# Banded product on four 64x64 tiles of TensorE, with half of the channels kept with swapped row halves, and a new order within a step

## The chip, the cores and the metric

The kernel runs on one core of one Trainium2 chip. The metric is the device time in microseconds; times of a kernel agree within a few tenths of a per cent. Matrix products run on TensorE (PE), which also loads weights (PEld in the profile); VectorE (DVE), ScalarE (ACT) and GpSimd (POOL) do the elementwise work, and SyncE (SP) starts the DMA transfers. All data is 32-bit floating point, and each matrix product of this type appears in the profile as a pair of records for the loads and a pair for the products (a transpose as one).

## The reference, cut to what matters

Two layers of the same form run one after the other on an image x of 512 x 512 positions with 64 channels:

```
xn    = layer_norm(group_norm(x))                       # 64 channels
left  = (xn @ Wl + bl) * mask * sigmoid(xn @ Wlg + blg)  # 128 channels
right = (xn @ Wr + br) * mask * sigmoid(xn @ Wrg + brg)
gate  = sigmoid(xn @ Wog + bog)
out[i, j, h] = sum over r with |r - i| <= 4 of left[r, i, h] * right[r, j, h]
x     = x + (layer_norm(out) * gate) @ Wo + bo
```

The sum over r is a matrix product for each of the 128 channels h: a band matrix (rows i, columns r, nine diagonals) times the columns j of `right`. `left` is needed only near the diagonal of the image.

## The kernel before, in words

**Tiling.** The 512 rows are cut into 9 blocks of 64 rows that overlap by 8. A block's 512 columns are taken as two halves of 256, which lie one above the other on the 128 partitions: partitions 0 to 63 hold the block's rows for columns of the left half, partitions 64 to 127 the same rows for the right half. A chunk is 128 columns of each half, so a layer has 18 chunks. A chunk is worked on in 16 steps, and each step takes one unit of 8 columns per half.

**What a unit goes through.** SP loads it (`load`, L390). Group norm is applied as a multiplication and an addition (`affine`, L426, on POOL, two instructions). DVE takes its statistics (`inner_stats`, L431). Every fourth step a `solve` (L577) turns the statistics of some units and outputs into reciprocal standard deviations: five small DVE instructions, then a chain of twelve on POOL. POOL subtracts and multiplies (`inner_norm`, L435). PE transposes the unit (`transposed`, L441), ACT copies the transposed unit to `zT` and adds 1, the row that carries the biases being folded in this way (`kept`, L460), and SP also writes it to DRAM (`later`). A step later, `right` (L487) multiplies `zT` with the weights of right and its gate in two calls of four columns: PE writes two banks of PSUM, ACT takes the sigmoid of one half of the channels into `sg`, and DVE multiplies it with the other half into `RO`, the array of 128 channels x 240 columns that holds the right side, and then, in place, the output of the band product.

**The left side.** At the head of a layer, the 36 near-diagonal columns go through the same way in five units (`left`, L497, at steps 3, 5, 7, 9, 11). ACT, POOL and DVE build the values in `sg`, and SP writes them from there into the DRAM array `left_of` in slabs of 16 channels, 108 transfers per layer. `left_of` has been filled with zeros, so reading it with another stride (`take_left`, L527) gives full 64 x 64 band matrices: tile `A`, 16 channels at a time, by two transfers of 256 KB.

**The band product.** `mix` (L539) takes 8 channels: for each of them, and each of the two halves, a product of a 64x64 matrix with 64x128 of `RO`. The lower half's products use rows and columns 0 to 63 of the array, the upper half's 64 to 127:

```
hh = (turn ^ e) * (HB // 2) + h
en.tensor.matmul(
    ph[part, hh, :], lhsT=A[part, :, h0 % HA + hh],
    rhs=R[part, (h0 + hh) // 2, :, hh % 2],
```

The result fills two banks; ACT copies the first half back into `RO`, DVE the second. A chunk has 16 such products, spread over its first ten steps as 2, 1, 2, 2, 1, 2, 1, 2, 2, 1; the other six steps have none.

**The output.** Some 14 steps after its band product starts, a unit of output has had its statistics taken (`out_stats`, L571, four DVE instructions) and solved; ACT normalises it in eight instructions into `on` (`norm`, L610; one buffer), PE turns it (`turned`, L641), PE and ACT make the output gate from the transposed input read back from DRAM (`gates`, L622; `recall`, L618), DVE adds the bias and multiplies by the gate into `ZH`, PE multiplies with Wo (`end`, L673), and DVE adds that to the residual `XR`, to which POOL has added the output bias (`biased`, L667). SP writes it. In layer 1, PE also sums the result for the next group norm (`sums`, L692, into its own bank `acc`).

**What sets the order.** Every instruction of a step is issued through the class `InOrder` (L365), which keeps program order on each engine; this is why nearly all profile rows carry L373, and why groups are told apart by their tiles. The order of a step in `layer` (L704) is: three output statistics, affines, first `right`, more statistics, `gates`, second `right`, `left`, `inner_norm`, `turned` with its multiplication, `transposed` and `kept`, `biased`, the rest of the statistics, `end`, `sums`, the solve, `norm` of the next output, and last the band products with their copies. Each engine takes its own part of this list, strictly in turn; SP does so too, with about nine transfers a step. PSUM has eight banks: two buffers of two banks (`two_banks`: both `right` calls, `transposed`, `mix`), and single banks (`one_bank`: `gates`, `turned`, `end`), three in layer 1 and four in layer 2.

Of the kernel before, what the change touches and what calls it, by code (L numbers as in the profile page):

```python
# [16 lines left out]
P = 128  # L17
WIN = 4
# [61 lines left out]
def tile_two_banded_layers(  # L80
# [28 lines left out]
    slab = S * (S + 2 * WIN) * HA  # L109
    size = H // HA * slab  # L110
# [271 lines left out]
    class Unit:  # L382
# [4 lines left out]
        def __init__(self, at: int, blk: Block = None, j: int = 0, near: int = None):  # L387
            self.at, self.blk, self.j, self.near = at, blk, j, near

# [70 lines left out]
    def kept(u: Unit):  # L460
        u.t = ztp.tile([P, JU // 2, P], F32, tag="zT", name="zT")
        to = u.t.rearrange("c k (n p) -> c n k p", n=2)
# [5 lines left out]
        if u.near is None:  # L468
            en.sync.dma_start(later[u.at], u.t)
# [5 lines left out]
    def projected(u: Unit, q: int, w: bass.AP):  # L475

        pr = two_banks().rearrange("p (e k h) -> p e k h", e=2, k=JQ // 2)
        for k in range(JQ // 2):
            for e in range(2):
                part = slice(e * D, (e + 1) * D)  # L480
                en.tensor.matmul(
                    pr[:, e, k, :], lhsT=u.t[part, q // 2 + k, :], rhs=w[part],
                    start=True, stop=True,
                )
        return pr

    def right(u: Unit, q: int, w: dict):  # L487
        pr = projected(u, q, w["right"]).rearrange("p e k h -> p (e k) h")
        sg = wk.tile([P, JQ, H], F32, tag="sg", name="sg", bufs=2)
        en.scalar.activation(sg, pr[:, :, H:], AF.Sigmoid)  # L490
        en.vector.tensor_tensor(
            RO[:, :, u.c + q : u.c + q + JQ, :],
            pr[:, :, :H].rearrange("p j (h t) -> p h j t", t=2),
            sg.rearrange("p j (h t) -> p h j t", t=2), ALU.mult,
        )

    def left(u: Unit, q: int, w: dict):  # L497
# [4 lines left out]
        sl = sg.rearrange("p j h -> p (j h)").rearrange("p (s j x) -> p s j x", j=JQ, x=HA)  # L502
        sv = sl.rearrange("p s (k e) x -> p e k s x", e=2)
        for e in range(2):
            en.scalar.activation(
                sv[:, e], pr[:, e, :, H:].rearrange("p k (s x) -> p k s x", x=HA), AF.Sigmoid
            )
        near = w["near"][:, n0 : n0 + JQ].unsqueeze(1).unsqueeze(3)
        en.gpsimd.tensor_tensor(sl, sl, near.broadcast_to([P, H // HA, JQ, HA]), ALU.mult)
        for e in range(2):  # L510
            en.vector.tensor_tensor(
                sv[:, e], pr[:, e, :, :H].rearrange("p k (s x) -> p k s x", x=HA), sv[:, e],
                ALU.mult,
            )
        for o, r, k, m in runs(n0, n0 + JQ):
            for n, b in enumerate(blocks):
                q0 = b.s // JQ
                at = n * size + (r * (S + 2 * WIN + 1) + k) * HA
                en.sync.dma_start(
                    strided(  # L520
                        left_of, at, (JQ * (S + 2 * WIN + 1) * HA, S // JQ), (slab, H // HA),
                        (1, m * HA),
                    ),
                    sl[q0 : q0 + S // JQ, :, o : o + m, :].rearrange("q s j x -> q s (j x)"),
                )

    def take_left(n: int, h: int) -> bass.AP:  # L527


        A = lp.tile([P, S, HA], F32, tag="A", name="A")  # L530
        at = n * size + h * slab + WIN * HA
        for e in range(2):
            en.sync.dma_start(
                A[e * S : (e + 1) * S].rearrange("p i h -> p (i h)"),
                strided(left_of, at, ((S + 2 * WIN) * HA, S), (1, S * HA)),
            )
        return A

    def mix(c: int, A: bass.AP, h0: int):  # L539


        j0 = c % 2 * (JC - JW)
        R = RO[:, :, j0 : j0 + JC, :]
        pb = two_banks()
        ph = pb.rearrange("i (h j) -> i h j", j=JC)
        for turn in range(2):
            for h in range(HB // 2):
                for e in range(2):
                    part = slice(e * S, (e + 1) * S)
                    hh = (turn ^ e) * (HB // 2) + h  # L550
# [431 lines left out]
```

## Time and profile before

| | |
|---|---|
| runs | 4960.42, 4958.66, 4958.12 us; median 4958.66 |
| span of the profiled execution | 4957.7 us |
| busy, share of the span | PE 84%, PE weight loads 71%, DVE 77%, ACT 74%, POOL 77% |
| DMA queue of SP | 899840 packets, 969.73 MB, 66.9% of 16 engines |
| band product, PE | 18432 records of 64x128, mean 277 ns (overlapping), 1154.3 us busy |
| projections, PE | 9360 records of 64x256, mean 405 ns, 1325.0 us busy |
| copies of the band product | 576 on ACT, 583 ns; 576 on DVE, 691 ns |
| zT copies on ACT | 542 of 128x512, 598 ns; 88 of 128x256, 385 ns |
| POOL, per unit | affine 1283 + 1282 ns, norm 1070 + 1055 ns, residual bias 1190 ns |

The median of the runs is 0.96 us above the span of the profiled execution. The shares are means over the whole span, which begins with some 300 us of group statistics and of zero filling, and has a drain and a refill between the layers, near 2500 to 2800 us; a stretch of the middle of a layer is the better guide. Busy times on PE count overlapping products once, so the pace of PE is read from the starts of its groups. A wait is written as the engine that waited, the releaser, the total in us, how often, and the longest.

### The profile page before, as it was taken

Reading aid. Unit: us, or ns where it says so; the run is one execution under the profiler, and the core shown is the slowest. Engines: PE = TensorE matmul, PEld = TensorE weight load, DVE = VectorE, ACT = ScalarE, POOL = GpSimd, SP = SyncE. Lnnn points to the kernel's source line nnn. Section 1 sums busy time; section 2 is a strip of 40 time slices with the busy share of each in tenths; the row PEclk is TensorE's granted clock in tenths of the full one; section 3 lists DMA queues with packets and bytes.
Section 4 is the critical chain, followed back from the end, with each engine's and each line's share of the span. In section 5 each row is a group of like instructions: output and inputs, shape, how many; then the busy total and the mean of one; then the engine's idle time right before and its main releaser. Section 6 shows DMA issues by size and latency. Waiting matters only on the chain. (4 is left out here: it accounts for less than half of the span.)

```text
span 4957.7 us, 173298 instructions
## 1 busy us (share of the span) xinstructions
PE 4186.4 (84%) x67090; PEld 3543.6 (71%) x67090; DVE 3836.3 (77%) x9635; ACT 3645.2 (74%) x8156; POOL 3826.5 (77%) x4739
## 2 busy tenths in 40 slices
PE   1036899999999999999974689999999999999998
PEld 0025788888888888888763577777777777777775
DVE  6855788888888888888766578888888888888876
ACT  0013788888888888888872378888888888888888
POOL 0037888888888888888534788888888998889853
PEclk6558999999999999999996899999999999999999
DMA  7844677777777777777653467777777777777765
GB/s 305 338 156 130 182 203 207 204 207 204 204 203 204 205 206 206 202 207 210 187 143 88 129 181 205 202 207 205 203 206 202 205 206 205 208 207 209 209 184 152
DMA packets 905343, 982.32 MB, mean 198 GB/s; under 512 B 114210, under 2 KB 641608, under 8 KB 900168
## 3 DMA queue, kind: packets, MB, share of 16 engines
q1 hardware_dynamic: 899840, 969.73, 66.9%
q8 instruction: 531, 8.70, 0.8%
q14 instruction: 292, 2.39, 0.2%
q10 hardware_dynamic: 4680, 1.50, 0.1%
HBM read 658.42 MB, written 312.46 MB: 196 GB/s over the span
## 5 line engine op out<-in xcount | busy, mean ns | idle before, releaser
L373 ACT ACTIVATE on<-RO,nm,rs 128x128 f32<-128x128 f32 x4608 | 1872.5, 496 | 130.1 <-POOL nm L373 110.3
L373 PE MATMUL banks<-pack,zT 64*128 64x256 f32 x9360 | 1325.0, 405 | 148.6 <-DVE RO L373 67.8
L373 PEld LDWEIGHTS banks<-pack,zT 64*128 64x128 f32 x9360 | 886.7, 194 | 517.6 <-DVE RO L373 220.1
L373 PE MATMUL banks<-RO,A 64*64 64x128 f32 x18432 | 1154.3, 277 | 12.7 <-ACT zT L373 12.7
L373 DVE TENSOR_TENSOR RO<-banks,sg 128x512 f32<-128x512 f32 x1152 | 789.9, 686 | 421.1 <-ACT sg L373 402.9
L373 PEld LDWEIGHTS banks<-RO,A 64*64 64x64 f32 x18432 | 1082.3, 183 | 38.6 <-ACT zT L373 15.2
L373 ACT ACTIVATE sg<-banks 128x512 f32<-128x512 f32 (+1 forms) x1188 | 695.0, 587 | 372.5 <-PE banks L373 288.6
L373 DVE BATCH_NORM_STATS2 sto<-RO 128x6 f32<-128x256 f32 x2304 | 842.8, 413 | 1.2
L373 DVE SCALAR_TENSOR_TENSOR ZH<-bank,pack,gate 128x448 f32<-128x448 f32 (+1 forms) x1152 | 738.4, 683 | 71.5 <-ACT gate L373 46.9
L373 DVE COPY RO<-banks 128x512 f32<-128x512 f32 x576 | 396.3, 691 | 487.6 <-ACT RO L373 487.0
L373 POOL TENSOR_TENSOR z<-z,gb 128x512 f32<-128x512 f32 x536 | 687.1, 1282 | 42.0
L373 PE MATMUL bank<-pack,ZH 128*64 128x64 f32 x18432 | 682.8, 229 | 6.1 <-ACT gate L373 5.6
L373 POOL TENSOR_TENSOR z<-z,ga 128x512 f32<-128x512 f32 x536 | 687.8, 1283 | 0.1
L373 POOL TENSOR_TENSOR z<-z,rs 128x512 f32<-128x512 f32 x586 | 618.0, 1055 | 46.0
L373 PEld LDWEIGHTS bank<-pack,ZH 128*64 128x64 f32 x18432 | 602.1, 141 | 48.2 <-ACT gate L373 9.6
L373 POOL TENSOR_TENSOR z<-z,sti 128x512 f32<-128x512 f32 x586 | 627.2, 1070 | 0.0
L373 ACT ACTIVATE gate<-bank 128x448 f32<-128x448 f32 (+1 forms) x1152 | 565.9, 543 | 81.1 <-PE bank L373 66.9
L373 PEld LDWEIGHTS bank<-ident,on 64*128 64x128 f32 x9216 | 409.7, 140 | 260.5 <-ACT gate L373 145.3
L373 PE MATMUL bank<-ident,on 64*128 64x64 f32 x9216 | 450.2, 227 | 137.9 <-ACT gate L373 107.3
L373 PE MATMUL bank<-zg,pack 64*128 64x448 f32 (+1 forms) x2304 | 559.5, 558 | 2.2 <-DMA zg<-later 1.5
L373 POOL TENSOR_TENSOR XR<-XR,pack 120x512 f32<-120x512 f32 (+1 forms) x352 | 418.4, 1190 | 160.6 <-DMA XR<-in_x_dram 58.9
L373 ACT COPY RO<-banks 128x512 f32<-128x512 f32 x576 | 333.5, 583 | 234.1 <-PE banks L373 234.0
(145 smaller groups left out, 3683.3 us busy)
## 6 DMA issues: line engine op xcount, KB each, us to landing
later<-zT SPq DMA_DIRECT2D x576, 256.0 KB
A<-left_of SPq DMA_DIRECT2D x576, 256.0 KB
zg<-later SPq DMA_DIRECT2D x576, 256.0 KB
z<-in_x_dram SPq DMA_DIRECT2D x576, 128.0 KB
z<-mid_x SPq DMA_DIRECT2D x576, 128.0 KB
gn_x<-in_x_dram SPq DMA_DIRECT2D x16, 4096.0 KB
XR<-in_x_dram SPq DMA_DIRECT2D x448, 112.0 KB
mid_x<-XR SPq DMA_DIRECT2D x448, 112.0 KB
```

Source lines behind the costliest of these rows:

```text
L373: return lambda *a, **k: tc.keep_in_program_order(f(*a, **k))
```

## The change

- `mix` takes 4 channels of the lower 64 and 4 of the upper 64 instead of 8 neighbours. The lower ones (s = 0) are multiplied as before; for the upper ones (s = 1) the products go to the other half's output partitions, so that the four 64x64 tiles are addressed in turn. Each s has a single bank of its own (`one_bank`, no longer `two_banks`). `mix` only issues the products; the copies are placed in the step by the caller.
- So that this adds up, the upper 64 channels of `RO` are kept with swapped row halves after one band product, and before it: `crossed` replaces `projected` for the right side and makes 8 products of 128 columns per call in place of 4 of 256. Half of them use weights that begin 64 columns further into `zT`, which therefore gets a third block, a copy of its first, by one more ACT instruction per unit in `kept`. The transfer to `later` takes only the first two blocks.
- The left side is kept as channel pairs: DVE writes it to `L9`, the last 36 columns of `RO`, and each of the four rows of diagonals goes out in 9 transfers when it is complete, with pieces of 18 values. `A` is read back in four transfers of 128 KB with pieces of 128 values.
- `right`, `gates`, `turned`, `norm`, `end` are cut into a PE part and the parts of ACT or DVE, and a step has a new order.

```
 def kept(u: Unit):
-    u.t = ztp.tile([P, JU // 2, P], F32, tag="zT", name="zT")
+    u.t = ztp.tile([P, JU // 2, P + S], F32, tag="zT", name="zT")
...
     if u.near is None:
-        en.sync.dma_start(later[u.at], u.t)
+        en.scalar.activation(
+            to[:, 2], u.pt[0][:, 0].rearrange("c (k p) -> c k p", p=S), AF.Identity, bias=1.0
+        )
+        en.sync.dma_start(later[u.at], u.t[:, :, :P])
...
+def crossed(u: Unit, q: int, w: bass.AP):
+    pr = two_banks().rearrange("p (e k h) -> p e k h", e=2, k=JQ // 2)
+    for k in range(JQ // 2):
+        for s in range(2):
+            for e in range(2):
+                part = slice(e * D, (e + 1) * D)
+                en.tensor.matmul(
+                    pr[:, e, k, :].rearrange("p (g s x) -> p g s x", g=2, s=2)[:, :, s],
+                    lhsT=u.t[part, q // 2 + k, s * S : s * S + P],
+                    rhs=w[part].rearrange("c (g s x) -> c g s x", g=2, s=2)[:, :, s],
+                    start=True, stop=True,
+                )
+    return pr
...
 def take_left(n: int, h: int) -> bass.AP:
+    A = lp.tile([P, HA // 2, S, 2], F32, tag="A", name="A")
+    q = HA // 4
+    for e in range(2):
+        for s in range(2):
             en.sync.dma_start(
+                A[e * S : (e + 1) * S, s * q : (s + 1) * q].rearrange("p h i t -> p h (i t)"),
                 strided(
+                    left_of, n * size + (s * H // 4 + h * q) * span + 2 * WIN,
+                    (H // 2 * span, S), (span, q), (1, 2 * S),
                 ),
             )
...
 def mix(c: int, A: bass.AP, h0: int) -> list:
+    R = RO.rearrange("p (s h) j t -> p s h j t", s=2)[:, :, h0 // 4 : h0 // 4 + q, j0 : j0 + JC]
+    L = A.rearrange("p (s h) i t -> p s h i t", s=2)[:, :, h0 % HA // 4 : h0 % HA // 4 + q]
+    ph = [one_bank().rearrange("i (h t j) -> i h t j", h=q, t=2) for s in range(2)]
+    for h in range(q):
+        for t in range(2):
+            for s in range(2):
+                for e in range(2):
+                    part, to = (slice(n * S, (n + 1) * S) for n in (e, e ^ s))
+                    en.tensor.matmul(
+                        ph[s][to, h, t, :], lhsT=L[part, s, h, :, t], rhs=R[part, s, h, :, t],
+                        start=True, stop=True,
+                    )
+    return [(R[:, s], ph[s].rearrange("i h t j -> i h j t")) for s in range(2)]
```

The new order of a step, with the engine that each entry occupies (transfers and conditions left out):

```
left; out_stats 0:3 (DVE); inner_norm (POOL)
right first half (PE); right_gate (ACT); gates (PE); right second half (PE)
affine (POOL); out_stats 3: (DVE); inner_stats (DVE); solve (DVE, POOL)   # solve every fourth step
gated (ACT); right_end first half (DVE); biased (POOL); turned (PE); right_gate second half (ACT)
transposed (PE); times_gate (DVE); affines of the next step after a solve (POOL); end (PE)
right_end second half (DVE); first mix (PE); norm 0:4 (ACT); kept (ACT); sums (PE)
copy of the first mix, s = 0 (ACT); ended (DVE); norm 4:8 (ACT); second mix (PE)
copy of the first mix, s = 1 (DVE); copies of the second mix (ACT, DVE)
```

## Prediction

> **What bounds the kernel now.** I read the page's first parts, then one 500 us stretch of the middle of layer 1 (busy times, waits), then the timeline of single steps on TensorE, ScalarE and GpSimd. Busy share first:
>
> ```profile
> 1500.00:2000.00 500.00, 481.14 (x8307) 421.74 (x8304) 403.75 (x1019) 418.52 (x934) 445.16 (x539) 0.99 0.72 205
> ```
>
> In steady state PE is busy 96%, POOL 89%, ACT 84%, DVE 81%, the DMA engines 72%, at full clock. Nothing has much room, so what a faster PE is worth depends on the next engine. One step with two band products (`mix`), and the start of the following one, on PE:
>
> ```profile
> 1509.70 1.13 PE L373 MATMUL banks<-pack,zT 64*128 64x256 f32 x8
> 1510.67 0.92 PE L373 MATMUL bank<-zg,pack 64*128 64x448 f32 x4
> 1511.42 1.03 PE L373 MATMUL banks<-pack,zT 64*128 64x256 f32 x8
> 1512.29 0.69 PE L373 MATMUL bank<-ident,on 64*128 64x64 f32 x16
> 1512.88 0.46 PE L373 MATMUL banks<-ident,z 64*128 64x64 f32 x8
> 1513.27 1.15 PE L373 MATMUL bank<-pack,ZH 128*64 128x64 f32 x32
> 1514.25 0.64 PE L373 MATMUL acc<-XR 120*64 120x65 f32 x16
> 1514.82 3.94 PE L373 MATMUL banks<-RO,A 64*64 64x128 f32 x64
> 1518.69 1.13 PE L373 MATMUL banks<-pack,zT 64*128 64x256 f32 x8
> ```
>
> From start to start: projection 0.97, gates 0.75, projection 0.87, turns 0.59, transposes 0.39, output product 0.98, sums 0.57, two band products 3.87: 8.99 us without a hole. So with band products PE is the bound; one costs 1.94 us, the rest 5.12. Without band products ACT is:
>
> ```profile
> 1589.51 0.60 ACT L373 ACTIVATE sg<-banks 128x512 f32<-128x512 f32 x1
> 1589.99 0.98 ACT L373 ACTIVATE gate<-bank 128x448 f32<-128x448 f32 x2
> 1590.84 0.61 ACT L373 ACTIVATE sg<-banks 128x512 f32<-128x512 f32 x1
> 1591.59 0.60 ACT L373 ACTIVATE zT<-banks 128x512 f32<-128x512 f32 x1
> 1592.08 3.21 ACT L373 ACTIVATE on<-RO,nm,rs 128x128 f32<-128x128 f32 x8
> 1595.20 0.58 ACT L373 ACTIVATE sg<-banks 128x512 f32<-128x512 f32 x1
> ```
>
> These steps repeat every 5.69 us and ACT has hardly a gap. A chunk is 16 steps: six with two products, four with one, six with none. It took 119.6 us in layer 1 (first projection at 1502.59 to the one at 1622.19) and 118.8 in layer 2 (3503.70 to 3622.48); 36 chunks make about 4290 of the 4957.7 us. The waits of the stretch:
>
> ```profile
> DVE RO L373 <- ACT RO L373: 61.1, 65, 1.3
> DVE RO L373 <- ACT sg L373: 30.0, 38, 2.0
> POOL rsqrt L373 <- DVE rs L373: 28.7, 17, 2.9
> ...
> PEld bank L373 <- ACT gate L373: 22.8, 21, 2.6
> ...
> PEld banks L373 <- DVE RO L373: 15.9, 43, 0.8
> ```
>
> The third line matters most: POOL hardly waits for anything else. Its work per chunk by the timeline, start to start: 16 steps of norm pair and residual bias (3.28), 16 affine pairs (2.61), 4 solves (4.54): 112.4 us. The change leaves that work alone, so a chunk can't get below 112.4.
>
> **The change, part by part.**
>
> *Band product.* It keeps its 16 products of 128 columns (32 record pairs) but spreads them over four tiles instead of two. If four run at once, 1.94 becomes 0.97. Bounds: no better than the output product's pace (32 pairs, two column tiles, 0.98); no worse than 1.94. I take 1.0, near the first, because that row already runs column tiles side by side and the projection row runs row tiles side by side. Gain on PE 0.94 per product, 16 per chunk: 15 us.
>
> *Projection of the right side.* Each of two calls per step has 16 pairs of 128 columns in place of 8 of 256: same streaming, twice the weight loads. Below: no cost. Above: every added load exposed at its busy time, 194 ns (1.6 us per call, or 0.8 when the two row tiles load side by side). Nearest row: the band product's pairs, also 128 columns in two tiles, 3.87/64 = 60 ns apart, so 16 take 0.97 against 0.87 to 0.97. I take +0.1 a call, +0.2 a step. PE's step is then 5.3 without products, 6.3 with one, 7.3 with two.
>
> The Trainium skill (TensorE: Matmul & The Clock Gate, "LDWEIGHTS") speaks against this part: a load takes its column count over 1.2 GHz, so 107 ns for 128 columns. By that, eight added loads, two side by side and none hidden, would cost 0.43 us a call, 14 us per chunk, all that the band product saves. The turns' row weighs against it: 16 pairs with 128-column loads start 0.59 to 0.75 us apart in all, 37 to 47 ns a pair, loads included.
>
> *Third block of zT.* ACT gets one more PSUM copy per unit, 128x256. The trace has that shape in the filling of a layer, 385 ns each, two back to back in 0.66: 0.33 us per step, 5.3 per chunk. With products PE has covered ACT's slack; without them it is bare.
>
> *Evacuation.* Copies stay 0.57 (ACT) and 0.69 (DVE) per product, but each half has its own bank, and the instruction list shows DVE's copy waiting for PE alone, no longer for ACT: the first wait above (61.1 per 500 us) goes. What is late next is PE itself.
>
> The skill (TensorEngine Tiling (Array Packing), "PSUM Bottleneck") warns that tiling speeds up TensorE, not the evacuation. If evacuation ruled, a product would cost DVE's 0.69 plus ACT's 0.57 in series, 1.26 instead of 1.0: 4 us more per chunk.
>
> *New order.* DVE begins a step with all statistics and the solve, then the first product with the sigmoid (`right_end`), gates, second `right_end`, residual, copies. The transposes need the bank pair that the first `right_end` frees, and the output product, the sums and all band products queue behind them on PE. So the step is
>
> T (transposes start) = max(3.45, tail + S + 0.78), and then 4.05 with two products, 3.0 with one, 2.0 with none.
>
> 3.45 is projection, latency, sigmoid, two gates and turns (0.97 + 0.25 + 0.5 + 0.98 + 0.75). Tail is DVE's copy after the previous step's last product: 0.8 after two products, 0.25 after one (the sums cover it), -0.3 after none. S is DVE's statistics: 0.36 per output record (4 as a rule, 7 in the chunk's first step), 0.84 per unit (one as a rule, none in the first step, two in the fourth, sixth and ninth), 0.9 for a solve (first, fifth, ninth). 0.78 is `right_end` with latency. In order from the chunk's first step I get 7.95, 6.9, 7.5, 8.85, 7.8, 8.3, 6.9, 7.5, 9.7, 6.9, where the trace has 9.6, 7.1, 9.0, 9.0, 7.1, 9.6, 7.0, 9.0, 9.0, 7.0: 78.3 against 83.4. The six steps without products are ACT's: 5.69 + 0.33 + 0.25 (ACT waits for the turns, as `on` has one buffer, and the zT copies no longer fill that gap) = 6.25, 37.5 against 36.2. Layer 1: 115.8 for 119.6. Layer 2 (no sums, four banks) gives 113 by the same sum, but POOL's chain from solve to solve holds it at about 115.2 for 118.8.
>
> POOL's stall: the solve now sits behind the norm and affine pairs (2.13 + 2.61 = 4.7 us into the step), while DVE is ready at 3.3 to 4.9, so the 6 us per chunk mostly go. The affines formerly put ahead of the solve come behind it; nobody needs them until the next step but one.
>
> The walk has no jitter. Done on the old kernel it gives 6 x 8.98 + 4 x 7.05 + 6 x 5.65 = 116 where the trace has 119.6, so it misses as much as it promises. I count half of its 3.7: 1.9 per chunk, 68 us in all.
>
> *Transfers.* `A` comes in 512 B packets instead of 4 KB (64 packets per step become 512), `later` goes out in 512 B instead of 2 KB (128 become 512). In 4870:4900, mostly 512 B packets, one took 37 ns (59% of 16 engines for 30 us, 7635 packets); in 440:510, 2 and 4 KB, 118 ns (49.4% of 70 us, 4705). Solving these two with the steady stretch gives about 26 ns for 512 B, 120 for 2 KB, 180 for 4 KB: no net cost. The other end, 37 ns against bare streaming at the 25 GB/s per engine of the statistics phase, adds some 18 engine-us per step: a share of 0.87 instead of 0.72, still under one. I take none. SP issues two more `A` starts per slab, 1.1 us per two steps, beside a queue that mostly waits for DVE (792 us).
>
> *Filling and draining.* In filling, ACT stood 33.9 and 33.4 us (layers 1 and 2) for `left_of` to leave `sg`; the left half now lies in RO, and 108 starts per layer become 36 (about 0.5 us each on SP). The pieces shrink to 72 B and rise from about 14,000 to 37,000 packets per layer; 330:420 puts small ones at some 14 ns, 9,216 a burst over 16 engines: 8 us, hidden. I take -10 per layer. Draining runs 16 products per layer at PE's pace (7.84 us steps with two): -12 per layer. Together -44.
>
> **Sum**, against the profiled 4957.7 (0.96 under the median; I use the median): 4958.7 - 68 - 44 = 4847; I say 4850.
>
> **Rivals.**
> - *The statistics-first order turns into the bound (ends slower).* Place: steps after two products, where copy, statistics, `right_end`, transposes, output product and product form one loop through DVE and PE. For it: three such steps already come out at 7.8 to 9.7 above, and inner statistics now need POOL's affines early. Against: in ten steps of 16 DVE is done by about 3.9. Price: 0.35 us in each of 16 steps is 5.6 per chunk against the 1.9 counted: 36 x 3.7 - 44 = +89, 5048. It decides once such waits pass 112/36/16 = 0.19 us a step.
> - *The four tiles don't overlap (the change doesn't do what it says).* Then PE keeps 1.94 and pays 0.2 a step, and DVE's late `right_end` stands in front: the walk becomes 115.8 + 15 = 130.8, and 36 x 11.2 less some 20 of the filling gives 5340. Against: the output product's row.
> - *The full walk holds*: 36 x 3.7 + 44 = 177, 4780; with POOL's floor everywhere (112.4) 4680.
> - *ACT eats it*: 16 x (6.25 + 0.57) = 109 per chunk, and with half of its present 18 us of waits (for PE and POOL, 77 in the 500 us) 118: about 4958.7 - 25, 4930 to 4990 with what filling does.
> - *DMA becomes the bound*: share 0.87 and late loads in two-product steps, 1 us each: 6 - 1.9 = +4.1 per chunk, 36 x 4.1 - 44 = +104, 5063.
>
> **How the numbers follow.** Forecast (4800 to 4925) 0.42; full walk or better 0.15; ACT eats it (4925 to 4990) 0.15, split evenly three ways; order 0.18; tiles 0.06; DMA 0.04. A change of 0.2% (10 us) is about what a measurement can tell. Faster 0.42 + 0.15 + 0.05 = 0.62, same 0.05, slower 0.05 + 0.18 + 0.06 + 0.04 = 0.33. Range 4745 to 5085: it holds all but the tile rival and the ends of the full walk and the order; the forecast's own is 4800 to 4925.
>
> **What would show it.** Two-product starts on PE about 1.0 us per product; projections within 0.1 of before; an extra 0.33 on ACT; DVE copies no longer released by ACT; POOL's wait for `rs` nearly gone; PE's wait for DVE `RO` grown at the transposes. Wrong if a product stays above 1.5, if PE waits over 0.19 us a step more than counted, or if the DMA share passes 0.9.

## The result and the profile after

The changed kernel took 4813.48 us (median of four, 4808.51 to 4821.8) against 4959.54 for the kernel before on the same chip: a ratio of 0.9706, 95% interval 0.9693 to 0.972. The profiled execution has a span of 4806.5 us (4957.7 before). The forecast was 4850 us, so the sign and the size are right; but the chunks gained more than forecast, and filling a layer lost where a gain had been counted. The starts of ScalarE's gate instructions, one pair per step, cut the two profiled executions into stretches:

| stretch, us | before | after | difference |
|---|---|---|---|
| start to the first gates of layer 1 | 529.3 | 539.7 | +10.4 |
| first to last gates of layer 1 | 2094.9 | 2015.3 | -79.6 |
| last gates of layer 1 to first of layer 2 | 263.8 | 272.9 | +9.1 |
| first to last gates of layer 2 | 2061.9 | 1970.7 | -91.2 |
| rest | 7.8 | 7.8 | 0 |

Inside a layer a chunk (mean of the third to the sixteenth, worked out from the same starts) went from 119.5 to 115.4 us in layer 1 and from 118.8 to 114.0 in layer 2.

Busy times of 500 us of layer 1 and of layer 2 after the change (PE, PEld, DVE, ACT, POOL, granted clock, share of the DMA engines, GB/s):

```profile
1500.00:2000.00 500.00, 457.04 (x9706) 403.37 (x9708) 426.71 (x1049) 443.56 (x1032) 459.09 (x552) 0.98 0.76 211
...
3500.00:4000.00 500.00, 421.79 (x8682) 370.06 (x8680) 445.28 (x1071) 442.84 (x1061) 462.06 (x564) 0.96 0.77 214
```

PE fell from 96% to 91% in layer 1 and is no longer ahead of GpSimd (POOL, 92%); ACT and DVE stand at 85 to 89%. Nothing is far behind, so the busy shares name no single bound. The granted clock is a little lower than before (0.99).

A step with two products on PE after the change (start, length, what):

```profile
1372.29 1.16 PE L373 MATMUL banks<-pack,zT 64*128 64x128 f32 x16
1373.29 0.92 PE L373 MATMUL bank<-zg,pack 64*128 64x448 f32 x4
1374.04 1.06 PE L373 MATMUL banks<-pack,zT 64*128 64x128 f32 x16
1374.93 0.67 PE L373 MATMUL bank<-ident,on 64*128 64x64 f32 x16
1375.42 0.43 PE L373 MATMUL banks<-ident,z 64*128 64x64 f32 x8
1375.79 1.15 PE L373 MATMUL bank<-pack,ZH 128*64 128x64 f32 x32
1376.87 1.29 PE L373 MATMUL bank<-RO,A 64*64 64x128 f32 x32
1378.09 0.69 PE L373 MATMUL acc<-XR 120*64 120x65 f32 x16
1378.71 1.16 PE L373 MATMUL bank<-RO,A 64*64 64x128 f32 x32
1379.79 1.16 PE L373 MATMUL banks<-pack,zT 64*128 64x128 f32 x16
```

7.50 us from projection to projection, again without a hole; 8.99 before. The two products take 1.22 and 1.08 in place of 1.94 each, the projections 1.00 and 0.89 in place of 0.97 and 0.87.

A step without products on ACT, up to the next one's first sigmoid:

```profile
1329.87 0.59 ACT L373 ACTIVATE sg<-banks 128x512 f32<-128x512 f32 x1
1330.35 0.96 ACT L373 ACTIVATE gate<-bank 128x448 f32<-128x448 f32 x2
1331.20 0.60 ACT L373 ACTIVATE sg<-banks 128x512 f32<-128x512 f32 x1
1331.74 1.71 ACT L373 ACTIVATE on<-RO,nm,rs 128x128 f32<-128x128 f32 x4
1333.34 0.85 ACT L373 ACTIVATE zT<-banks 128x512 f32<-128x512 f32 x2
1334.08 1.67 ACT L373 ACTIVATE on<-RO,nm,rs 128x128 f32<-128x128 f32 x4
1335.64 0.59 ACT L373 ACTIVATE sg<-banks 128x512 f32<-128x512 f32 x1
```

5.77 us although `zT` now has two copies (x2): each instruction follows the one before it, and the small holes of the old step are gone.

The waits of 1500 to 2000 us (who waited, for whom, us, times, longest):

```profile
DVE RO L373 <- PE bank L373: 44.2, 56, 1.6
PE banks L373 <- DVE RO L373: 33.5, 34, 2.7
ACT RO L373 <- PE bank L373: 32.7, 31, 2.8
...
POOL rsqrt L373 <- DVE rs L373: 14.5, 17, 1.9
```

DVE's copies no longer wait for ACT (61.1 before) but for PE; PE waits for DVE's `right_end` at the transposes; POOL's wait for the solve is half of its 28.7. Over the whole execution the wait at the transposes is now the largest on PE (busy, mean ns, idle before and its releasers), before and after:

```profile
L373 PE MATMUL banks<-ident,z 64*128 64x64 f32 x4336 | 249.2, 230 | 95.7 <-DVE RO L373 65.1 <-POOL rsqrt L373 21.2 <-POOL z L373 4.8
L373 PE MATMUL banks<-ident,z 64*128 64x64 f32 x4336 | 254.1, 233 | 359.2 <-DVE RO L373 336.9
```

One wait is gone that the prediction doesn't price. In the old order the normalisation of the output (`on`) came to wait for the `nm` that POOL's solve makes; over the whole execution before:

```profile
ACT on L373 <- POOL nm L373: 110.3, 74, 3.2
```

After the change it is 1.5 us, twice. It stood in the fourteenth step of a chunk (n = 13, without products): 7.68 us in layer 1 before, in the mean of 14 chunks, and 5.79 after.

### The profile page after: what moved, and what is told of

Its sections match the earlier page's. It is cut to its first block, busy times and chain, and to the rows that moved or that the text cites. A ratio compares the mean times of both kernels' runs of the same rounds, so it can differ in the third digit from the quotient of the medians.

```text
span 4806.5 us, 193543 instructions
## 1 busy us (share of the span) xinstructions
PE 3796.6 (79%) x76306; PEld 3293.0 (69%) x76306; DVE 3929.9 (82%) x9635; ACT 3708.4 (77%) x8732; POOL 3817.1 (79%) x4739
## 5 line engine op out<-in xcount | busy, mean ns | idle before, releaser
L373 PEld LDWEIGHTS banks<-pack,zT 64*128 64x128 f32 x18576 | 1251.3, 195 | 549.5 <-ACT zT L373 288.9
L373 PE MATMUL banks<-pack,zT 64*128 64x128 f32 x18576 | 1365.6, 289 | 272.8 <-ACT zT L373 222.6
L373 DVE TENSOR_TENSOR RO<-banks,sg 128x512 f32<-128x512 f32 (+1 forms) x1188 | 795.3, 673 | 228.3 <-POOL sg L373 116.2
L373 PE MATMUL bank<-RO,A 64*64 64x128 f32 x18432 | 706.0, 292 | 3.9 <-ACT RO L373 2.4
L373 DVE COPY RO<-bank 128x512 f32<-128x512 f32 x576 | 398.4, 692 | 310.6 <-PE bank L373 307.3
L373 PEld LDWEIGHTS bank<-RO,A 64*64 64x64 f32 x18432 | 582.0, 142 | 43.0 <-ACT RO L373 4.1
L373 ACT ACTIVATE zT<-banks 128x512 f32<-128x512 f32 (+1 forms) x1084 | 463.5, 481 | 139.6 <-PE banks L373 128.9
L373 ACT COPY RO<-bank 128x512 f32<-128x512 f32 x576 | 333.2, 579 | 282.3 <-PE bank L373 282.1
L373 PE MATMUL banks<-ident,z 64*128 64x64 f32 x4336 | 254.1, 233 | 359.2 <-DVE RO L373 336.9
L373 DVE BATCH_NORM_STATS2 sti<-z 128x6 f32<-128x128 f32 x2344 | 500.5, 280 | 15.2 <-POOL z L373 14.2
```

Of the source, the lines that this page charges most:

```text
L373: return lambda *a, **k: tc.keep_in_program_order(f(*a, **k))
```

## The experiments

Step lengths are means over 14 chunks of layer 1, worked out from the starts of the gate instructions; n is the place in the chunk, 0 to 9 being the steps with products; "six others" is the sum of n = 10 to 15. The row of the forecast is the walk in the prediction.

| kernel | n = 0 to 9 | sum | six others | chunk, layer 1 | chunk, layer 2 |
|---|---|---|---|---|---|
| before | 8.9 7.1 9.0 9.0 7.1 9.6 7.1 9.0 9.0 7.1 | 82.8 | 36.7 | 119.5 | 118.8 |
| forecast | 7.95 6.9 7.5 8.85 7.8 8.3 6.9 7.5 9.7 6.9 | 78.3 | 37.5 | 115.8 | 115.2 |
| after | 8.34 6.82 7.52 8.84 10.29 7.93 6.84 7.49 10.13 6.47 | 80.7 | 34.8 | 115.4 | 114.0 |
| two_tiles | 9.12 7.34 8.38 9.71 7.97 9.09 7.33 8.39 10.45 6.79 | 84.6 | 34.8 | 119.3 | 115.2 |
| old_order | 8.84 6.45 9.83 8.93 6.53 10.90 7.15 9.85 8.96 6.51 | 83.9 | 38.8 | 122.7 | 126.3 |
| affine_after | 8.14 6.96 7.52 8.84 7.46 13.36 6.83 7.49 9.47 6.91 | 83.0 | 36.6 | 119.6 | 118.6 |
| solve_late | 7.64 6.87 7.50 8.84 8.28 10.02 6.84 7.49 9.09 6.45 | 79.0 | 36.7 | 115.7 | 114.8 |
| no_bias | 8.18 6.82 7.49 8.84 7.46 8.21 6.82 7.49 9.86 6.46 | 77.6 | 35.7 | 113.3 | 111.9 |
| third_twice | 7.78 6.87 7.82 8.79 9.86 8.16 6.88 7.82 10.17 6.79 | 80.9 | 37.1 | 118.1 | 115.8 |

### Two tiles at a time

```
-        for h in range(q):
-            for t in range(2):
-                for s in range(2):
+        for s in range(2):
+            for h in range(q):
+                for t in range(2):
                     for e in range(2):
```

> The changed kernel, but a band product issues first its eight channel-halves of the straight tiles, then its eight of the crossed ones, so that two tiles are addressed at a time instead of four. Same work, same layout, same step order. Theory (the product's pace on TensorE carries the gain, and it lies on the path): a product goes back from about 1.03 to 1.9 us, 16 per chunk and 36 chunks give about +520 us, 5250 to 5360 in all, slower than the kernel before. Rival (the step order carries the gain and the products have slack): at most 4860.

Measured: 4906.05 us (4902.0 to 4907.91), ratio to before 0.9896 (0.9879 to 0.9912). Neither theory had it. The edit undid only about half of what it was meant to undo: a product took 1.59 us in layer 1 and 1.39 in layer 2 (median, start to start), not 1.9. The starts of the single records say why. Before, two product records start within 5 to 10 ns and the next two some 107 ns after them, and a product spans 1832 ns from its first to its last start. After, four start within about 25 ns and the next four some 90 ns after them: 969 ns. Here the straight half runs in twos, but the first crossed records start while the last straight ones are still in flight, and the product spans 1393 ns. So tiles that are next in line in another corner of the array do overlap here; the whole gain was measured only with an order that alternates them all the time.

What a slower product costs can be read all the same. In layer 1 it added some 0.86 us to a step with two products (7.52 to 8.38, 8.84 to 9.71) and 0.5 to one with one: all on the path. But n = 4 got 2.3 us shorter, so of 16 x 0.42 = 6.7 us a chunk paid 3.9. In layer 2, of 16 x 0.36 = 5.8 it paid 1.2.

### The channel pairs alone

The kernel before with the new `left`, and `A` read back as channel pairs; still two tiles, old order:

```
-        A = lp.tile([P, S, HA], F32, tag="A", name="A")
+        A = lp.tile([P, HA // 2, S, 2], F32, tag="A", name="A")
...
-                        ph[part, hh, :], lhsT=A[part, :, h0 % HA + hh],
+                        ph[part, hh, :], lhsT=A[part, (h0 % HA + hh) // 2, :, hh % 2],
```

> The kernel before with one part of the change alone: the left side kept as channel pairs (weights of the band product 8 bytes apart in place of 64), written by the same 36 transfers of small pieces per layer. Two tiles at a time, old step order, no swapped halves. Theory (weights that lie closer are loaded faster: the loads' mean falls from 183 to about 135 ns, and this, not the four tiles, makes the first part of the product's gain): a product goes from 1.94 to 1.4 to 1.6 us; the layer 1 chunk, where TensorE bounds, loses 16 x 0.35 to 0.5, down to GpSimd's 111 plus waits, some 115; filling costs 30 us more per layer: 4850 to 4920. Rival (the load's distance doesn't matter and only the crossing made two_tiles faster): product stays 1.9, 4985 to 5020 with the filling.

Measured: 4995.03 us (4992.63 to 5002.84), ratio 1.0086 (1.0072 to 1.0099). The rival holds. The weight loads did get shorter (183 to 133 ns in 1500 to 2000 us), but the product only went from 1.94 to 1.90 us, and chunks stayed at 119.4 and 118.4. Loads shorter by 50 ns are worth 0.04 us of a product here. What the new form of the left side brings by itself is a longer filling: first gates at 549.4 us (529.3 before), 282.7 between the layers (263.8), together +39 of the 41 us by which the run is longer.

### The new product in the old order

The step of the kernel before, with the new pieces (`right`, `right_gate` and `right_end` in a row, both copies behind each product), and the product's banks as a pair again:

```
+                first_half, second_half = mix(c, A[c, h0 // HA], h0)
+                en.scalar.copy(*first_half)
+                en.vector.tensor_copy(*second_half)
...
-        ph = [one_bank().rearrange("i (h t j) -> i h t j", h=q, t=2) for s in range(2)]
+        pb = two_banks()
+        ph = [
+            pb[:, s * 512 : (s + 1) * 512].rearrange("i (h t j) -> i h t j", h=q, t=2)
+            for s in range(2)
+        ]
```

> The new product, the new layout of left and right side and the third block of zT, but the step order of the kernel before, with both copies right behind each product and the product's two banks as one pair again. Theory A (the product's pace carries the gain and the order little): 4780 to 4850. Theory B (the old order can't use the faster product, because copies and statistics then stand between the products and the next transposes): 4900 to 4980. Product on TensorE about 1.0 us in both.

Measured: 5178.38 us (5175.27 to 5185.37), ratio 1.0449 (1.0434 to 1.0465): the fast product, in the old order, is slower than the slow one. Theory B, and beyond its range. A two-product step on PE:

```profile
1460.32 2.07 PE L373 MATMUL banks<-RO,A 64*64 64x128 f32 x64
1464.16 1.16 PE L373 MATMUL banks<-pack,zT 64*128 64x128 f32 x16 [1.76 <-DVE RO L373]
```

and on ACT:

```profile
1459.64 3.27 ACT L373 ACTIVATE on<-RO,nm,rs 128x128 f32<-128x128 f32 x8
1462.81 1.05 ACT L373 COPY RO<-banks 128x512 f32<-128x512 f32 x2
1465.37 0.60 ACT L373 ACTIVATE sg<-banks 128x512 f32<-128x512 f32 x1 [1.51 <-PE banks L373]
```

Two products are done in 2.07 us, at 1462.4, but ACT is still in its eight instructions for `on` and copies only at 1462.8, DVE after it; the next projection needs the bank pair and waits 1.76 us, and then ACT waits 1.51 us for the projection. The loop through ACT, DVE and PE, which the slow product had covered, is now the step. The new order takes it apart: `on` in two halves with a copy between them, banks of their own, no chain from ACT to DVE. The chunks cost only part of the 221 us: the first gates come at 560.5 us and 292.9 lie between the layers, together 60 us more than before. Why the chunk became even longer than before (122.7 and 126.3) is not settled: this kernel also has the third copy on ACT and the doubled projections. The other half of the cross, the new order with the old product, was not run; two_tiles, with products of 1.59 and 1.39 us, is the nearest.

### Where the solve stands in DVE's order, and what slows it

In the changed kernel n = 4 and n = 8, the steps with a solve, are the ones above the forecast, in layer 2 even 11.7 and 11.5 us. DVE and POOL in such a step of layer 2:

```profile
3670.91 0.88 DVE L373 BATCH_NORM_STATS2 sti<-z 128x6 f32<-128x128 f32 x4
3671.69 0.99 DVE L373 TENSOR_SCALAR var<-sti 128x32 f32<-128x32 f32 x1
3672.61 0.18 DVE L373 SCALAR_TENSOR_TENSOR var<-sto,pack 128x32 f32<-128x32 f32 x1
3672.83 1.20 DVE L373 TENSOR_SCALAR var<-var 128x32 f32<-128x32 f32 x1
3673.94 0.17 DVE L373 TENSOR_SCALAR nm<-sto 128x32 f32<-128x32 f32 x1
3674.06 1.23 DVE L373 TENSOR_SCALAR rs<-var 128x64 int32<-128x64 int32 x1
3675.21 0.68 DVE L373 TENSOR_TENSOR RO<-banks,sg 128x512 f32<-128x512 f32 x1
```

```profile
3671.38 1.27 POOL L373 TENSOR_TENSOR z<-z,ga 128x512 f32<-128x512 f32 x1
3672.73 1.26 POOL L373 TENSOR_TENSOR z<-z,gb 128x512 f32<-128x512 f32 x1
3673.95 1.29 POOL L373 TENSOR_TENSOR z<-z,ga 128x512 f32<-128x512 f32 x1
```

Three TENSOR_SCALARs of 0.2 us take 0.99, 1.20 and 1.23, and each ends when a POOL instruction ends (3672.65, 3673.99, 3675.24). `right_end` comes 3 us late, and PE stands 3.9 us in front of the transposes. Then its clock drops (PE, PEld, DVE, ACT, POOL, clock, DMA share, GB/s):

```profile
3672.00:3676.00 4.00, 0.13 (x5) 0.00 (x0) 3.96 (x7) 2.01 (x5) 3.84 (x4) 1.00 0.89 269
3676.00:3678.00 2.00, 1.97 (x38) 1.93 (x40) 1.67 (x3) 0.87 (x2) 1.75 (x5) 0.60 0.77 201
3678.00:3680.00 2.00, 2.00 (x40) 1.76 (x36) 0.69 (x1) 0.00 (x0) 1.58 (x6) 0.55 0.90 238
```

At half the clock the output product and the band product, 1.15 us each, took 1.97 and 1.80: another 1.5 us. In layer 2 half clock comes about twice a chunk (31 times in 16 chunks), for 3.41 or 6.83 us each time.

First the cause of the long TENSOR_SCALARs. In solve steps POOL gets its affine pair behind the solve, so that it stands still while DVE does the small instructions:

```
+            if t % 4 or t <= NU:
                 for u in affines.pop(t, []):
                     affine(u, en.vector if u.at < NU + 4 else en.gpsimd)
...
                     solve(w, us, os, st, so)
+            for u in affines.pop(t, []):
+                affine(u, en.gpsimd)
```

> The changed kernel, but in solve steps GpSimd gets its affine pair behind the solve, so it waits while VectorE does the small instructions of the solve. Theory (VectorE's TENSOR_SCALARs on SBUF stand still until a running GpSimd instruction ends): their means fall from 554, 514 and 325 ns towards 280, 240 and 195, TensorE's wait for RO in front of the transposes falls from 337 to below 200 us, the fifth and ninth step of a chunk lose 2 us each, and GpSimd pays about 1.2 us of waiting in each of three solves: 4740 to 4810. Rival (the durations have another cause): means unchanged, 4813 or slower by up to 36 x 3.6 = 130.

Measured: 4977.79 us (4974.83 to 4980.2), ratio 1.0042 (1.0027 to 1.0057). The durations do what the theory says; groups of the changed kernel (busy, mean ns):

```profile
L373 DVE TENSOR_SCALAR var<-sti 128x32 f32<-128x32 f32 (+4 forms) x146 | 78.8, 540 | 0.3
L373 DVE TENSOR_SCALAR var<-var 128x32 f32<-128x32 f32 x144 | 74.0, 514 | 5.0
L373 DVE TENSOR_SCALAR rs<-var 128x64 int32<-128x64 int32 (+4 forms) x160 | 51.1, 319 | 0.5
```

and with POOL standing still:

```profile
L373 DVE TENSOR_SCALAR var<-var 128x32 f32<-128x32 f32 x144 | 37.7, 262 | 4.9
L373 DVE TENSOR_SCALAR rs<-var 128x64 int32<-128x64 int32 (+4 forms) x160 | 31.8, 199 | 0.6
L373 DVE TENSOR_SCALAR var<-sti 128x32 f32<-128x32 f32 (+4 forms) x146 | 28.4, 194 | 0.3
```

n = 4 fell to the forecast's length, 10.29 to 7.46 us. The price went elsewhere: the late affines hold up DVE's next inner statistics (idle before `sti<-z` 298.9 us in all, 15.2 in the changed kernel), n = 5 rose from 7.93 to 13.36, and n = 13 from 5.79 to 7.63. PE's wait for DVE at the transposes, expected below 200 us, rose from 336.9 to 491.0, and the theory's time, 4740 to 4810, was wrong.

Then the same stall avoided on DVE's side: the block with the solve moves behind the first `right_end` and the multiplication with the gate.

```
-            if t % 4 == 0:
-                ...
-                    solve(w, us, os, st, so)
             if t in outs:
                 gated(outs[t])
             if t in units:
                 right_end(units[t], 0)
...
                 times_gate(outs[t], w)
+            if t % 4 == 0:
+                ...
+                    solve(w, us, os, st, so)
```

> The changed kernel, but the solve is issued behind the first right-side product and the gate product of VectorE, not ahead of them. Theory (the late first right-side product of solve steps delays the transposes and everything behind them on TensorE): the fifth and ninth step go from 10.2 to about 8 us in layer 1 and from 11.5 to about 7.6 in layer 2; GpSimd's own work, 112.4 us a chunk, then bounds: 3.0 less per chunk in layer 1 and 1.6 in layer 2, 18 chunks each, so 4730, between 4690 and 4775. The TENSOR_SCALARs stay slow. Rival (these steps are held by GpSimd's chain from solve to solve already): 4800 to 4830.

Measured: 4857.61 us (4851.92 to 4866.9), ratio 0.9802 (0.9787 to 0.9817): slower than the changed kernel, and neither the theory nor the rival had it. n = 4 fell again, to 8.28 us in layer 1 and 6.69 in layer 2, and n = 5 rose, to 10.02 and 10.93. The reciprocal deviations come later: PE's waits at the transposes for POOL's `rsqrt` and `z` went from 17.8 to 71.8 us over the execution, those for DVE from 336.9 to 163.3. The chunk hardly moved (115.7 and 114.8). Of the 48 us by which the profiled execution is longer, filling is 14 (first gates at 547.8 us, 278.4 between the layers), the draining after a layer's last unit 18, the chunks the rest. The stall of the solve steps is real, but taken away there, the time comes back one step on.

### GpSimd's work taken away

In every kernel so far POOL's chunk was 111 us (110.9 to 111.4, chunk less its waits) and the rest waits: 8.3 and 7.6 before, 4.3 and 2.9 after. That looks like a bound. To test it, POOL's addition of the output bias is left out in both kernels:

```
             if t in outs:
-                biased(outs[t], w, stats)
+                pass
```

> The changed kernel without GpSimd's addition of the output bias to the residual: this part of the computation is left out, 16 instructions of some 1.16 us a chunk. Theory (a chunk lasts as long as GpSimd's own work, 111.1 us in all six kernels so far, plus its waits for the solve): GpSimd has 92.5 us left, so the next engines decide, which without their waits have 105.8 (TensorE, layer 1) and 101.9 (VectorE, layer 2); chunks of about 108 and 105 us, 4525 in all, between 4450 and 4620. Rival (the loop of VectorE and TensorE behind two-product steps holds the chunk and GpSimd only fits in): 4760 to 4815.

> The kernel before with the same addition left out. Theory: TensorE without its waits has 114.5 (layer 1) and 110.2 us (layer 2) a chunk, so chunks fall from 119.5 and 118.8 only to about 117 and 114: 4825, between 4780 and 4900, and the change under study would then be worth some 300 us in place of 146. Rival (GpSimd alone is the bound before as well): 4670 or less.

Measured: the changed kernel 4769.54 us (4745.39 to 4781.3), ratio to before 0.9617 (0.9582 to 0.9652); the kernel before 4937.36 (4935.16 to 4939.6), 0.9963 (0.9948 to 0.9977). So some 18 us of POOL work a chunk are worth 44 and 18 us in all (in the changed kernel the whole chunks gained 63 and filling lost 20): for the changed kernel the theory falls and the rival holds; for the kernel before neither range had it. POOL's waits grew to 20.4 and 18.9 us a chunk. In the kernel before, layer 1 did not move at all (119.5 both times), so POOL is not its bound; PE, at 114.8 us without its waits, is the nearest, which no run tests. In the changed kernel layer 1 came down to the forecast's walk, every product step within 0.45 us: that fits the loop of DVE and PE as its bound, with POOL adding 2.1 us. In layer 2 the chunk stopped at 111.9, with PE waiting 4.4 us a chunk for `zg` and POOL 3.8 for `z`, both transfers; the DMA engines, at 0.78 of their time, may come next, which was not tested.

### The filling

The left side's 36 transfers per layer come in four bursts of nine, 1024 pieces of 72 bytes each. Three kernels change only them. left_one writes just the first of nine row blocks (`blocks[:1]`; 4 transfers a layer, not the 8 of its expectation); left_spread puts the transfers in a list and issues at most five at the end of a step; left_late issues the first block's at once and the others two a step. The edit of the last, cut:

```
-                    en.sync.dma_start(
+                    (later_left if n else first_left).append((
                         strided(
...
+            for v in first_left + later_left[:2]:
+                en.sync.dma_start(*v)
+            first_left.clear()
+            del later_left[:2]
```

> The changed kernel, but only one of the nine row blocks of the left side is written to DRAM (the other eight stay zero: this part is left out), so 8 transfers per layer's filling in place of 36 bursts of small pieces. Theory (bursts of nine transfers at 1.1 to 1.6 us each on SyncE's queue hold up later's transfers and so ScalarE's zT): each filling loses 15 to 25 us, 4765 to 4785. Rival (the chain of left units through ScalarE, GpSimd and VectorE sets the pace): 4805 to 4815.

> The changed kernel, but the transfers of the left side are issued at the end of a step, at most five a step, in place of nine at once near its head. Theory (their place on SyncE's queue matters): half of what left_one gains, 4780 to 4805. Rival (their number and piece size matter, not the place): 4810 to 4830.

> The changed kernel, but at the end of a step: the transfers of the left side that the first row block needs go at once, those of the other eight blocks two a step, up to about the twentieth step. Theory (nine transfers at once saturate the DMA engines with 72-byte pieces, 30 ns each in the mean where the median is 12, and hold up loads and zT; spread out they hide): two thirds of the 78 us of left_one, 4760, between 4735 and 4785. Rival (the pieces cost their 36,864 x 30 ns over 16 engines, 69 us a layer, wherever they stand): 4790 to 4815.

| kernel | time, us | ratio to before | first gates of layer 1 | between the layers |
|---|---|---|---|---|
| before | | | 529.3 | 263.8 |
| after | 4813.48 | 0.9706 (0.9693 to 0.972) | 539.7 | 272.9 |
| left_one | 4735.39 | 0.9555 (0.9541 to 0.957) | 504.1 | 231.1 |
| left_spread | 4794.86 | 0.9675 (0.966 to 0.9689) | 530.3 | 263.7 |
| left_late | 4752.25 | 0.9595 (0.9581 to 0.9608) | 511.4 | 239.4 |

The other eight blocks' pieces cost 36 and 42 us a layer, more than left_one's theory said; chunks are the same in all of them (115.3 to 115.6 and 114.0 to 114.1). left_spread, within its theory's range, won back 19 of left_one's 78 us, and left_late 61, as its theory had it. Two stretches of the filling of the changed kernel (the last two numbers are the DMA share and GB/s; a packet counts where it starts, so a share can pass 1):

```profile
375.00:405.00 30.00, 9.83 (x105) 8.05 (x103) 10.77 (x24) 6.02 (x16) 13.11 (x20) 0.68 0.99 59
405.00:440.00 35.00, 14.30 (x152) 12.93 (x150) 12.91 (x32) 7.98 (x20) 12.56 (x19) 0.64 1.15 60
```

and with the late blocks spread (left_late):

```profile
375.00:405.00 30.00, 21.07 (x256) 19.74 (x256) 21.20 (x51) 13.37 (x35) 22.72 (x27) 0.75 0.68 97
405.00:440.00 35.00, 24.66 (x352) 21.42 (x352) 15.97 (x42) 12.45 (x26) 27.80 (x33) 0.71 0.83 137
```

The DMA engines are full while moving only 60 GB/s, and all five engines do about half of the work, or somewhat more. From 310 to 560 us a packet of up to 72 bytes took 12 ns in the median in both, but 30.5 in the mean in the changed kernel and 13.2 in left_late (1222 and 535 us over all engines), and 27.4 in left_spread: the pieces are dear when many transfers meet. Each burst of nine also held SyncE's own queue for 9.9 to 15.1 us, with the next `later` behind it; over the filling of layer 1 the 36 starts took 50.4 us, in left_late 32.1, a few at a time. The runs do not separate the dear packets from this wait in the queue. Spread out, most of it hides. left_late is the fastest kernel here that leaves nothing out, 4752.25 us (4746.53 to 4758.72).

### The third block, twice

```
             en.scalar.activation(
                 to[:, 2], u.pt[0][:, 0].rearrange("c (k p) -> c k p", p=S), AF.Identity, bias=1.0
             )
+            en.scalar.activation(
+                to[:, 2], u.pt[0][:, 0].rearrange("c (k p) -> c k p", p=S), AF.Identity, bias=1.0
+            )
```

> The changed kernel with ScalarE's copy of the third block of zT done twice, so that its price can be read: one more 128x256 copy per unit, some 0.33 us from start to start. Theory (steps without products last as long as ScalarE's own list, 5.76 us, without a gap; in steps with products ScalarE has slack): the six steps without products go to 6.1, the others stay, 2.0 us a chunk: 4813 + 36 x 2.0 = 4885, between 4860 and 4905. Rival A (ScalarE bounds everywhere): 16 x 0.33 x 36 = 190, 5000. Rival B (GpSimd's waits take it in): 4815 to 4835.

Measured: 4875.59 us (4874.5 to 4876.18), ratio 0.9831 (0.9814 to 0.9847), as the theory has it. The six steps without products went from 5.8 to 6.18 us, their sum by 2.3, those with products by 0.3. If the first copy costs what the second does, the third block costs the change about 62 us.

## Why the prediction was right, and where it was not

**Band product, 1.94 to 1.0 us: right.** 1.17 us in layer 1 and 1.03 in layer 2, in the median. Four tiles do run at once. That it would be worth 15 us a chunk "on PE" was never the sum, and two_tiles shows what it is worth in the new order: 0.42 us per product were 3.9 us a chunk in layer 1 and 1.2 in layer 2.

**Projection, +0.1 a call: too much.** 0.92 to 0.95 us in the mean of layer 1; pairs_only points the same way, with 50 ns shorter loads that gain 0.04 us per product. The estimate of 0.43 us a call for eight added loads, worked out from the load time in the Trainium skill (TensorE: Matmul & The Clock Gate, "LDWEIGHTS") as if none were hidden, isn't seen.

**Third block, +0.33 a step: about right**, and bare only without products, as said: third_twice reads 0.38 us in each of those steps and 0.03 in the others. **Evacuation: right.** The chain from ACT to DVE is gone, and in the 7.50 us step two products follow with no wait for a copy. The warning of the Trainium skill (TensorEngine Tiling (Array Packing), "PSUM Bottleneck"), that copying out may become the bottleneck, does not come true in this step: its products take 1.22 and 1.08 us, under the 1.26 of the two copies in series.

**The walk of the new order: right step by step, its total partly by luck.** 115.8 us for layer 1, 115.4 measured; 115.2 for layer 2, 114.0 measured. Nine of ten product steps of layer 1 are within 0.45 us of it. Two terms were off and nearly cancelled: the fifth step, 7.8 counted and 10.29 measured, where POOL's running instructions stretch DVE's solve; and the steps without products, 37.5 counted and 34.8 measured. There the 0.25 us that ACT was to wait for the turns doesn't exist, and of the 0.75 us from the second sigmoid to the next instruction in the old step 0.54 is left. In layer 2 the number came by another road: the walk alone gave 113 and POOL's chain was to hold it at 115.2, but what stands above the walk are two solve steps of 11.7 and 11.5 us.

**The step that failed is the halving.** "The walk has no jitter ... I count half of its 3.7: 1.9 per chunk, 68 us in all." The measured chunk gain is 4.0 and 4.8 us, the whole walk and some more. The 3.6 us by which the walk had missed on the old kernel were taken for jitter that the new one would have too. They were no jitter: 2.0 us of them lay in the old n = 13 (7.68 against 5.65), where ACT waits for `nm`, and 0.65 in n = 5. The new order took that wait away, and n = 13 is 5.79: 1.9 of layer 1's 4.0 us. In solve_late, whose solve ends late again, the wait is back, 117.1 us in 75 times, and n = 13 is 6.95. no_bias, at the walk's own lengths, shows hardly any jitter in the product steps. The rival "the full walk holds" (4780) is what the chunks did.

**POOL's stall, "mostly go": half of it went** (28.7 to 14.5 us in the 500 us of layer 1). The 112.4 us floor was a good count (111.1), but as a bound it was too strong: layer 2 came within 3 us of it and did not stand on it, since no_bias took 18 us of it away and the chunk lost 2.1.

**Transfers, no net cost: right in the chunks** (share 0.72 to 0.76 in layer 1, TensorE hardly waits for any), **wrong in the filling.** There the sum said -10 us a layer, with 36 starts of about 0.5 us each on SyncE and a burst of 8 us, hidden, from 14 ns a piece; it is +10 and +9, with starts of 1.4 us and 30 ns a piece. ACT's wait for `left_of` did go, but a larger one for `later` came: 43 us in 300 to 520 us, 17 before. The Trainium skill (DMA: Bandwidth & Descriptors, "Specifications") puts full line rate at 512 B and more and says that smaller ones are read, changed and written back. The 72-byte pieces at 60 GB/s are far from that rate, but no run here shows the reading back, and the same pieces took 13.2 ns in left_late, so their size alone does not make the 30. The draining, from a layer's last unit to its last gates, gained 15.7 and 17.8 us where 12 each were counted; the 16 steps that hold the last products, on which the count rested, gave 5.6 and 9.3 of it, the 13 behind them the rest. Filling and draining together: -14 against -44.

So the forecast was 37 us too high: it gave the chunks some 70 us too little (68 counted; 64 and 76 measured in the 16 whole chunks of each layer) and the ends of the layers 30 too much.

**The rivals.** "The order turns into the bound" named the right place: PE's wait for DVE in front of the transposes rose by 272 us over the execution. It did not decide because the walk had counted most of it. The tiles overlap; ACT did not eat the gain; the DMA engines are not the bound, though they may be the next in layer 2.

## What to carry to other kernels

A walk through the new order, step by step with the loop's own terms, held within half a microsecond in nine of ten product steps; don't discount it for jitter that hasn't been shown, but look in which steps it misses on the old kernel. A faster product needs an order that lets the next engine use it: here the same new pieces, with their added copies and loads, lost 221 us in the old order and won 146 in the new one. And "work plus waits adds up to the chunk" holds for every engine and proves no bound: take some of the work away and see whether the chunk follows.

## What the runs showed of the hardware

- In the solve step shown, three TENSOR_SCALARs of DVE between SBUF tiles that began while a POOL instruction ran ended only with it: 0.2 us became 0.99 to 1.23; with POOL standing still (affine_after) their means are 0.19 to 0.26. In solve_late also a SCALAR_TENSOR_TENSOR with two inputs in SBUF did (1.32 us at 3705.20). DVE's statistics in the same steps were not stretched (`sto<-RO` 411 ns after, 413 before). The Trainium skill has a rule that fits (SBUF — State Buffer, "Who interferes with whom"): DVE's second pair of ports is GpSimd's only one, and whoever holds it keeps it for a whole instruction. The prediction had taken these instructions at their old length, measured while POOL was waiting for them.
- A product in two tiles and one in the two others overlap where they meet: 1393 ns from the first start to the last, between 1832 and 969.
- Half clock came for 3.41 or 6.83 us at a time. In layer 1 of the changed kernel (16 whole chunks) it followed within 1.6 us on 14 of 20 waits of PE of 2.2 to 2.8 us and on 4 of 11 of about 1.7 us; in layer 2 it came with all 31 of 2.7 to 4.0 us. In layer 2 of the kernel before it came ten times, though no wait there was above 2.3 us. So the length of one wait does not settle it.
- Weights 8 bytes apart load in 133 ns, 64 bytes apart in 183 (the records of the 64x64 loads in pairs_only and before); the product changed from 1.94 to 1.90 us.
